# A larger allowed lateness for the planned order of VectorE and ScalarE in a four-layer graph kernel

## The chip, the cores and the metric

The kernel runs on one core of one Trainium2 chip. The metric is the device time of one execution in microseconds, as the median over the runs of one kernel. The profile comes from one further execution. In it PE is TensorE's matmuls, PEld its weight loads, DVE is VectorE, ACT is ScalarE, POOL is GpSimd and SP the engine that issues most of the loads.

## The reference

The input is x (4096 x 64) and adj (4096 x 4096, about one entry in 128 is 1, the others 0). Four graph layers follow each other, each as `x = x + layer(relu(layernorm(x)), adj)`:

```python
# layer 0: weights from the rank of a neighbour in its row
out = w @ (h @ weight) + bias          # w = mask * 0.5 ** (k - pos) where pos > 0
# layer 1: attention
h, q, k = lorentz_linear(...)           # 64 columns each
att = adj * sigmoid((2 + 2 * qm @ k.T) / att_scale + att_bias)
support = att @ h
out = support / sqrt(|-inner(support)|)
# layer 2: two gated graph convolutions, each with m = adj @ (x @ W)
# layer 3: hyperbolic: num = A @ (gamma * X), den = A @ (gamma - 1), alpha = sum(A),
#          then norms, artanh and tanh per row
```

## The kernel before

**A fast and a general program.** `fast_kernel` holds adj as 8-bit floats in on-chip memory for all four layers (tiles `A8`), which is exact only if every entry is 0 or 1. Whether that is so is tested as the kernel runs: the generator `checks` loads 128 pieces of adj of 128 x 1024 in 32-bit floats (`whole`, 512 KB each; the first few are shared with the conversion to 8 bits), and one VectorE instruction for each piece counts entries that are neither 0 nor 1 (a scalar_tensor_tensor with an accumulator, which the trace lists as a second, short instruction, DVE_READ_ACCUMULATOR). Every 16 tests their counts are added up; behind the last one a matmul `flag_ps` and a copy make the `flag`, and only if it is above 0 does `general_kernel` run afterwards. The tests can stand anywhere before the end; nothing but the reading of the flag at the end waits for their values.

**The planner.** The order of the instructions is written by a small planner, `Weave`, while the program is built. It keeps a planned clock for every engine (`weave.t`), books every instruction with a cost (`Engine.cost`: on VectorE 0.13 us plus 1.09 ns an element, 0.08 more with an accumulator) and remembers when each tile is ready. The main line of the program, scores, sums and evacuations, is issued directly (`V`, `S_`); side work is given as generators (`DV`, `AC`) that are put in where there is room. Side work is in `weave.work`, of which the first two pieces are looked at; the tests are in `weave.back`, which is looked at after those and not at all while `weave.quiet` is set. Two places put side work in:

- `fill`, called before each direct instruction of VectorE and ScalarE: an operation goes ahead of it if its planned end is not after the moment at which the direct one is ready, plus `weave.late`.
- `draw`, called between groups of matmuls: an operation of VectorE or ScalarE is issued if its planned end is at most 0.4 us plus `weave.late` past TensorE's planned clock.

```python
if self.e in "DA":
    w.fill(self.e, w.ready(self.e, ins, outs) + w.late)      # a direct instruction, L791

go = begin + op.dur <= now + self.LAG["P"] + self.late       # draw, L726
```

**Layer 0** (`stream0`) and the first quarter of layer 1 come first, to about 308 us in the trace. **Layer 1's corner part** is the function `rest` in `stream1`: for three quarters q of the rows and two halves c, 16 steps i, 96 steps in all. A step is four score matmuls of a 64 x 64 corner (`score4`), two sigmoids on ScalarE and one multiply by adj on VectorE (`weigh`, tile `sig`), and four matmuls that sum (`sum4`); the sums of a step are issued behind the scores of the third step after it. `sig` and `whole` share six buffers (`b4`). In this part `depth[0]` is 1: the load of one further piece is issued when a test is. Beside it runs the post-processing of the quarter before (`post1`: row statistics, layer norm, splits), as side work.

**Layer 2** (`layer2`, two convolutions, 475 to about 677 us) is planned with `depth[0]` 4 and takes tests where VectorE has room, until `weave.quiet` is set ahead of the last evacuation. **Layer 3** (`layer3`) sums eight units of 512 rows. It begins with the halves that are ready; when the last S tiles are there (`DONE` has (4, NQ - 1)) all tests that are left are issued at once, ahead of everything else on VectorE:

```python
weave.quiet = False
while weave.back and weave.back[0][1].e == "D":
    weave.issue(weave.back[0])
```

Then each unit is evacuated (`take3`), its row statistics are made (`head3`), and norms, artanh and tanh follow (`post3`): for units 3 to 5 and 0 to 2 in groups of three, for units 6 and 7 singly. `last3` does unit 7, after which nothing is left for TensorE. Helpers record nearly all operations, so L785 in the profile is any operation of the planner's engines, and L984 any matmul.

Of the kernel before, what the change touches and what calls it, by code (L numbers as in the profile page):

```python
# [796 lines left out]
def fast_kernel(ctx: ExitStack, tc: tile.TileContext, t: dict, out: bass.AP, flag: bass.AP):  # L797
# [24 lines left out]
    weave = Weave()  # L822
    free = weave.free

    def one(name):
        return weave.take(1, lambda: psp.tile([P, CW], F32, tag="one", name=name, bufs=8))

    def several(names_):
        return [one(n) for n in names_]

    def b2(name, shape=(P, QB, D), dtype=F32):
        return b2p.tile(list(shape), dtype, tag="b2", name=name)
# [148 lines left out]
    def mm(o, lhsT, rhs, start=True, stop=True):  # L981
        weave.wait(names(lhsT, rhs), names(o))
        book_pe(o, lhsT, rhs, 4 if lhsT.dtype == F32 else 1)
        nc.tensor.matmul(o, lhsT, rhs, start=start, stop=stop, skip_group_check=True)  # L984
# [340 lines left out]
    def load1(q):  # L1325
        if q < NQ:
            qd[q] = [b2("qd", (P, CW)) for _ in range(2)]
            for c in range(2):
                for half in (slice(0, D), slice(D, P)):
                    Y_.dma_start(qd[q][c][half, :], q_spill[q][c * D:(c + 1) * D, :])  # L1330

    def score(q, i, c):

        kb = kT[i // 4][:, (i % 4) * P:(i % 4 + 1) * P]
        ps = several(("score", "score"))
        for j in range(2):
            half = slice(j * D, (j + 1) * D)
            mm(ps[j], kb[half, :], qd[q][c][half, :])
        return ps
# [3 lines left out]
    def score4(q, i, c):  # L1343

        kb = kT[i // 4][:, (i % 4) * P:(i % 4 + 1) * P]
        ps = several(("score", "score"))
        for j, (r, h) in enumerate(corners):
            mm(ps[j // 2][h, :], kb[r, h], qd[q][c][r, :])
        return ps

    def sum4(acc, i, g):

        for k, (r, h) in enumerate(corners):
            b = 2 * i + k % 2
            mm(acc[k // 2][h, :], S1[b // QB][r, b % QB, :], g[r, k % 2, :],
               start=i == 0, stop=i == NB // 2 - 1)

    def weigh(q, i, c, ps):

        g = b4p.tile([P, 2, CW], F32, tag="b4", name="sig")  # L1360
        for j in range(2):
            S_.activation(g[:, j, :], ps[j], AF.Sigmoid, bias=att_add, scale=att_mul)
            free(ps[j])
        v = g.rearrange("p k (j n) -> p k j n", n=P)
        a = A8[q][i].rearrange("p k (j c n) -> p k c j n", c=2, n=P)[:, :, c]
        V.tensor_tensor(v, v, a, ALU.mult)
        return g
# [9 lines left out]
    def stream1():  # L1377

        acc, behind = [], []

        def add(c, q, i, gs):
            if i == 0:
                acc.append(one(f"acc{c}"))
            for j in range(2):
                b = 2 * i + j
                mm(acc[c][j * D:(j + 1) * D, :], S1[b // QB][:, b % QB, :], gs[c][:, j, :],
                   start=i == 0, stop=i == NB // 2 - 1)

        def add_behind(more=()):
            q, i, gs = behind.pop(0)  # L1390
            for c in (0, 1):
                add(c, q, i, gs)
                if more:
                    more.pop(0)()
                weave.draw(weave.quiet)

        def turn(q, i, later=None):
            if q == 0 and i % (QB // 2) == 0:
                weave.until((1, i // (QB // 2)), DONE)
            weave.quiet = (1, NQ - 1) not in DONE  # L1400
            weave.late = 2.0 if weave.quiet else 0.8
            gs = ahead[:] if (q, i) == (0, 0) else []
            for c in range(len(gs), 2):
                ps = score(q, i, c)
                if later is None:
                    gs.append(weigh(q, i, c, ps))
                else:
                    later.append(lambda q=q, i=i, c=c, ps=ps: gs.append(weigh(q, i, c, ps)))
                weave.draw(weave.quiet or c == 1)
            behind.append((q, i, gs))  # L1410
            if i == 8:
                load1(1)

        def rest():

            q0, i0, gs = behind.pop(0)

            def last():
                add(1, q0, i0, gs)
                weave.finish()  # L1420
                weave.add(post1(q0, acc[:]))
                acc.clear()

            sums = [lambda: add(0, q0, i0, gs), last]

            def close(q, c, ps):
                if c == 0:
                    halves[q] = b2("agg", (P, CW))
                    weave.add(evac4(halves[q], ps, c))
                else:  # L1430
                    weave.finish()
                    weave.add(post1(q, ps))

            def sums_of(q, c, i, g):
                if i == 0:
                    acc[:] = several(("acc0", "acc1"))
                sum4(acc, i, g)
                if i == NB // 2 - 1:
                    close(q, c, acc[:])
                    acc.clear()  # L1440

            def pop():
                sums.pop(0)()
                weave.draw()

            for q in range(1, NQ):
                for c in (0, 1):
                    for i in range(NB // 2):
                        g = weigh(q, i, c, score4(q, i, c))
                        weave.draw(False)  # L1450
                        sums.append(lambda q=q, c=c, i=i, g=g: sums_of(q, c, i, g))
                        if len(sums) > 3:
                            pop()
                        if (c, i) == (1, 0):
                            load1(q + 1)
            while sums:
                pop()

        for q in range(1):
            for i in range(0, NB // 2, 2):  # L1460

                later = []
                turn(q, i)
                turn(q, i + 1, later)
                while len(behind) > 2:
                    add_behind(later)
                for go in later:
                    go()
                if len(behind) > 1:
                    add_behind()  # L1470
        weave.until((1, NQ - 1), DONE)
        weave.quiet, weave.late = False, 0.8
        rest()

    X, halves = {}, {}
# [1 line left out]
    def evac4(a, acc, c):  # L1477

        own, other = [slice(0, D), slice(D, P)][::1 - 2 * c]
        t = b2("mt", (P, CW))  # L1480
        yield AC.activation(t, acc[0], AF.Copy)
        free(acc[0])
        yield DV.tensor_tensor(t, acc[1], t, ALU.add)
        free(acc[1])
        yield AC.activation(a[own, :], t[other, :], AF.Copy)
        yield DV.tensor_tensor(a[own, :], t[own, :], a[own, :], ALU.add)

    def post1(q, acc):
        if q in halves:
            a = halves[q]  # L1490
            yield from evac4(a, acc, 1)
        else:
            a = yield from evac(acc)
        X[q] = b2(f"X{q}")
        yield SY.dma_start(flat(X[q]), x_spill[q])
        sup = b2("sup")
        ps = yield from to_nm(a)
        sq = b2("sq")
        yield AC.activation(sq, ps, AF.Square)
        yield AC.activation(sup, ps, AF.Copy)  # L1500
        free(ps)
        s = stat("space", QB)
        yield DV.tensor_reduce(s, sq[:, :, 1:], AX.X, ALU.add)
        yield DV.tensor_tensor(s, s, sq[:, :, 0], ALU.subtract)
        a = stat("abs", QB)
        yield DV.tensor_scalar(a, s, -1.0, 1e-8, op0=ALU.mult, op1=ALU.max)
        yield DV.tensor_tensor(s, s, a, ALU.max)
        r = yield from rsqrt(s)
        yield DV.tensor_tensor(sup, sup, rows(r), ALU.mult)
        yield DV.tensor_tensor(X[q], X[q], sup, ALU.add)  # L1510

        g = b2("g0")
        yield from relu_ln(X[q], g)
        yield from split3(g, 1.0, *parts(2, q), psum=False)
        DONE.add((2, q))
        gT = b2("gT", (P, CW))
        yield from transpose4(g, gT)
        yield from spill2(q, 0, gT)
# [443 lines left out]
    lead[0] = math.inf  # L1962
    depth[0] = 1
    stream1()
    depth[0] = 4
    for step in range(2):
# [89 lines left out]
```

## Time and profile before

| | |
|---|---|
| median of the runs | 793.5 us (793.33 to 793.5) |
| the profiled execution, its own time | 794.03 us |
| its span in the trace | 792.2 us |
| PE busy | 751.9 us (95%) |
| DVE busy | 636.0 us (80%) |
| ACT busy | 435.8 us (55%) |
| tests of adj on VectorE | 128 |
| granted TensorE clock, mean | 0.989 |

The span is what the trace covers; the profiled execution's own time holds 1.8 us more around it. Busy shares are means over stages that differ: in the slices of the page TensorE stands at nine tenths or more nearly throughout, and VectorE between five and nine tenths.

### The profile page before, as it was taken

The page shows a single profiled execution, that of the slowest core. Times are in us where ns is not written, and L with a number is a line of the kernel's source. Part 1 is how long each engine was busy: PE and PEld are TensorE (multiplying, and loading weights), DVE is VectorE, ACT ScalarE, POOL GpSimd, SP SyncE. Part 2 cuts the span into 40 slices and gives each one's busy share as a digit, 9 for nine tenths or more (in the row PEclk, how much of TensorE's full clock was granted, in tenths as well). Part 3 has the DMA queues.
Part 4 walks back from the last instruction along what each step waited for, and adds up shares of the span by engine and source line. Part 5 has one row for each costly group of instructions (what it writes and reads, how often), then busy time and mean ns, then how long its engine had stood idle before and what let it go on. Part 6 is the DMA issues. An engine that isn't in the chain of part 4 may idle for free.

```text
span 792.2 us, 13872 instructions
## 1 busy us (share of the span) xinstructions
PE 751.9 (95%) x5241; PEld 364.6 (46%) x5262; DVE 636.0 (80%) x1442; ACT 435.8 (55%) x765; POOL 62.0 (8%) x129
## 2 busy tenths in 40 slices
PE   6899999999999999999999999999999999999980
PEld 2334444444543433333333334434444354899980
DVE  5886867778779888998988988857978688768886
ACT  5555556555557678898899882041220345532243
POOL 4332232231000000000000000000000000000000
PEclk9999999999999999999999999999999999999995
DMA  9999999999610013010010027987779620003001
GB/s 202 155 188 178 222 164 193 222 164 207 202 49 26 14 67 94 1 55 28 2 54 1 2 65 235 321 252 245 257 258 363 188 80 28 1 2 134 2 22 37
DMA packets 44106, 98.64 MB, mean 125 GB/s; under 512 B 5120, under 2 KB 20608, under 8 KB 44032
## 3 DMA queue, kind: packets, MB, share of 16 engines
q1 hardware_dynamic: 25888, 78.98, 29.2%
q0 software_dynamic: 15984, 14.56, 19.6%
q10 hardware_dynamic: 2160, 4.14, 1.4%
q8 instruction: 43, 0.70, 0.4%
q14 instruction: 31, 0.25, 0.1%
HBM read 136.06 MB, written 5.24 MB: 178 GB/s over the span
## 4 chain that ended last, share of the span: by engine, by line
PE 79%; DVE 12%; ACT 3%; DMA 2%; issue 2%; SPq 0%; ACTq 0%; DVEq 0%
PE acc L984 47%; PE score L984 13%; PE cnt L984 12%; DVE n L785 2%; PE rz L984 2%; DVE ss L785 2%; PE ps_l L984 1%; DMA whole<-in_adjT 1%; PE ps_t L988 1%; DVE whole L785 1%; DVE sig L785 1%; DVE nt L785 1%; PE ih L984 1%; ACT sig L785 1%; DMA x<-in_x 1%
## 5 line engine op out<-in xcount | busy, mean ns | idle before, releaser
L785 ACT ACTIVATE sig<-score,fatt_add,fatt_mul 128x512 f32<-128x512 f32 x256 | 182.8, 776 | 31.4 <-PE score L984 25.6
L785 DVE TENSOR_TENSOR sig<-sig,A 128x1024 f32<-128x1024 f32 x128 | 155.2, 1222 | 24.2 <-ACT sig L785 22.3
L785 ACT ACTIVATE w<-cnt 128x512 int16<-128x512 f32 x198 | 111.4, 595 | 90.2 <-PE cnt L984 87.4
L785 DVE SCALAR_TENSOR_TENSOR whole<-whole 128x1024 f32<-128x1024 f32 x128 | 153.0, 1218 | 9.4 <-DMA whole<-in_adjT 8.8
L984 PE MATMUL acc<-sig,S 64*64 64x512 f32 (+1 forms) x896 | 130.8, 592 | 1.4 <-DVE sig L785 1.2
L984 PE MATMUL score<-qd,kT 64*64 64x512 f32 (+1 forms) x896 | 131.6, 594 | 0.0
L984 PEld LDWEIGHTS <-hm 128*128 128x128 bf16 x768 | 73.5, 98 | 92.5 <-issue 9.3
L984 PE MATMUL acc<-A,hm 128*128 128x512 fp8e4 x512 | 115.2, 379 | 0.0
L984 PE MATMUL cnt<-A,ftri 128*128 128x512 fp8e4 x256 | 97.4, 383 | 7.1 <-ACT A L785 5.8
L984 PE MATMUL cnt<-A,fupd 128*128 128x512 fp8e4 x248 | 94.8, 382 | 5.7 <-DVE w L785 2.1
L984 PE MATMUL acc<-S,A 128*128 128x196 bf16 x1024 | 88.5, 246 | 1.3 <-DVE S L785 1.3
L984 PEld LDWEIGHTS <-A 128*128 128x128 fp8e4 x1024 | 87.0, 97 | 2.2 <-DVE S L785 1.5
L984 PEld LDWEIGHTS score<-qd,kT 64*64 64x64 f32 (+1 forms) x896 | 41.1, 140 | 67.6 <-issue 57.5
L785 DVE TENSOR_SCALAR w<-cnt 128x512 int16<-128x512 f32 x58 | 40.1, 691 | 39.9 <-PE cnt L984 38.5
L984 PE MATMUL acc<-w,hm 128*128 128x512 bf16 x235 | 70.4, 379 | 1.2 <-DVE hm L785 0.4
L984 PEld LDWEIGHTS acc<-sig,S 64*64 64x64 f32 (+1 forms) x896 | 36.8, 133 | 74.9 <-issue 47.7
L868 POOL DMA_DIRECT2D A<-in_adjT x111 | 59.9, 542 | 127.2 <-DMA A<-in_adjT 126.0
L984 PEld LDWEIGHTS <-lo 128*64 128x64 bf16 x768 | 39.6, 109 | 49.3 <-issue 18.5
L984 PE MATMUL acc<-A,lo 128*64 128x512 fp8e4 x512 | 57.9, 380 | 0.0
L785 ACT ACTIVATE mt<-acc 64x512 f32<-64x512 f32 (+1 forms) x32 | 19.0, 592 | 64.1 <-PE acc L984 63.6
L984 PEld LDWEIGHTS <-ftri 128*128 128x128 bf16 x256 | 24.8, 98 | 45.5 <-issue 21.4
L984 PEld LDWEIGHTS <-fupd 128*128 128x128 bf16 x248 | 24.3, 98 | 37.9 <-issue 13.3
(190 smaller groups left out, 618.2 us busy)
## 6 DMA issues: line engine op xcount, KB each, us to landing
whole<-in_adjT SPq DMA_DIRECT2D x128, 512.0 KB, 6.8
A<-in_adjT POOLq DMA_DIRECT2D x111, 128.0 KB, 13.7
qd<-qs SPq DMA_DIRECT2D x16, 128.0 KB, 3.7
mx<-gs SPq DMA_DIRECT2D x16, 128.0 KB, 8.4
xT<-gs SPq DMA_DIRECT2D x8, 256.0 KB, 7.5
x<-in_x SPq DMA_DIRECT2D x6, 256.0 KB, 6.1
xs<-x SPq DMA_DIRECT2D x4, 256.0 KB, 5.9
qs<-qT ACTq DMA_DIRECT2D x4, 256.0 KB, 4.6
```

Of the source, the lines that this page charges most:

```text
L785: return fn(*args, **kw)
L868: nc.gpsimd.dma_start(A8[q][b // 2][:, b % 2, :], a)
L984: nc.tensor.matmul(o, lhsT, rhs, start=start, stop=stop, skip_group_check=True)
L988: nc.tensor.transpose(o, src, ident)
```

## The change

One number. After the first quarter of layer 1, and before the corner part begins, `weave.late` is set to 1.2 instead of 0.8. It is not set again, so the value holds for everything that is planned after that line, the corner part, layer 2 and layer 3. What the engines compute is the same; only the order in which VectorE's and ScalarE's instructions stand, and with it that of the loads of `whole`, can differ.

```diff
         weave.until((1, NQ - 1), DONE)
-        weave.quiet, weave.late = False, 0.8
+        weave.quiet, weave.late = False, 1.2
         rest()
```

## The prediction

> **What bounds the kernel now.** I read the busy times stage by stage first, then TensorE's waits, then the chain that ended last, then VectorE's timeline in two places.
>
> The stages (start and end in us; busy us of PE, PEld, DVE, ACT, POOL, each with its count; clock; DMA share; GB/s) are the corner part, the last tests with the sums beside them, the rest of layer 3, and what follows TensorE's last matmul:
>
> ```profile
> 308.00:475.00 167.00, 167.00 (x1540) 59.67 (x1532) 148.92 (x203) 150.02 (x219) 0.00 (x0) 1.00 0.09 27
> 719.70:736.00 16.30, 15.61 (x182) 15.28 (x182) 14.27 (x28) 1.03 (x6) 0.00 (x0) 1.00 0.47 162
> 736.00:769.90 33.90, 33.89 (x398) 33.62 (x397) 30.62 (x138) 12.40 (x46) 0.00 (x0) 1.00 0.04 14
> 769.90:792.20 22.30, 0.00 (x0) 0.00 (x0) 15.06 (x89) 9.31 (x21) 0.00 (x0) 0.61 0.10 33
> ```
>
> See in it: TensorE is never idle in the corner part, while VectorE has 18 us to spare there. At the end it is the reverse: TensorE stops at 769.9 and VectorE works on. The same table for the instructions on `whole` (DVE alone; two counts are one test) says where the tests of adj run: 3 in the corner part, 66 from 475 to 640, 1 to 719.7, and 11 from 719.7 to 736:
>
> ```profile
> 308.00:475.00 167.00, 3.68 (x6) 0.00 (x0) 0.00 (x0) 1.00 0.09 27
> 475.00:640.00 165.00, 78.89 (x132) 0.00 (x0) 0.00 (x0) 1.00 0.76 255
> 640.00:719.70 79.70, 1.23 (x2) 0.00 (x0) 0.00 (x0) 1.00 0.09 28
> 719.70:736.00 16.30, 12.95 (x22) 0.00 (x0) 0.00 (x0) 1.00 0.47 162
> ```
>
> TensorE's waits from 470 us on (total, times, longest):
>
> ```profile
> PE acc L984 <- DVE S L785: 1.3, 1, 1.3
> PE flag_ps L984 <- DVE n L785: 0.7, 1, 0.7
> PE acc L984 <- DVE sig L785: 0.2, 1, 0.2
> ```
>
> So TensorE itself can gain little. The chain of waits shows what the last tests cost (start, us, what):
>
> ```profile
> 719.24 0.84 DVE S L785 x2
> 720.08 5.16 DVE whole L785 x9
> 725.24 0.48 issue
> ...
> 725.83 7.71 DMA whole<-in_adjT
> 733.63 1.24 DVE whole L785 x2
> ```
>
> From 719.2 the chain runs over VectorE almost without a break to the end: the 11 tests hold it from 719.99 to 734.89, 14.9 us with 1.9 us of waits for loads, and everything that layer 3 wants from it is late by that much. The first sums' addition, `n<-n,acc`, ready before 724, runs at 735.18.
>
> VectorE in the corner part, where no post-processing runs:
>
> ```profile
> 416.38 1.23 DVE L785 TENSOR_TENSOR sig<-sig,A 128x1024 f32<-128x1024 f32 x1 [0.49 <-ACT sig L785]
> 418.10 1.23 DVE L785 TENSOR_TENSOR sig<-sig,A 128x1024 f32<-128x1024 f32 x1 [0.49 <-ACT sig L785]
> 419.81 1.23 DVE L785 TENSOR_TENSOR sig<-sig,A 128x1024 f32<-128x1024 f32 x1 [0.49 <-ACT sig L785]
> ```
>
> A step is 1.717 us, and 0.49 us idle stands in front of every multiply, with no test in any gap.
>
> [...]
>
> **The change, step by step.**
>
> (1) *Why 0.8 lets no test in.* A test is put before a multiply if its planned end is at most `late` past the moment the multiply is ready. Planned: test 0.13 + 1.09e-3 x 1024 + 0.08 = 1.326 us, multiply 1.246, step on TensorE 8 x 0.215 = 1.72, two sigmoids 1.32. VectorE is then free 1.72 - 1.246 = 0.474 us before the multiply (0.49 in the trace, so the plan holds). A test needs 1.326 - 0.8 = 0.526: just too much, in every step. With 1.2 it needs 0.126.
>
> (2) *How many go in.* After a test VectorE is 0.852 behind, then 0.378, then 0.096 ahead (under 0.126), then 0.474 again: one test in three steps. Walking over the idle gaps of the corner part in the trace (16.2 us behind the sigmoids, in 39 gaps) with 1.33 us a test, I get 12 places; post-processing that is pushed back, and tests that were there anyway, take some. I take **10 more (6 to 12)**.
>
> (3) *What they cost there.* Each adds 1.15 us to VectorE (its start-to-start time, 719.99 to 721.14), in idle time. The multiply behind it is up to 0.7 us late (1.15 less the gap). Who waits for that: sums of a step are issued behind the scores of the third step after it. The multiply of 356.52 ends at 357.75, its sums start at 359.97: 2.2 us to spare, so nothing until the last steps. There the last multiply is waited for already (0.2 us); one test in front adds up to 0.7. I take +0.5. Each test also issues one load on SP's queue, past the q and x loads of the next parts, which are asked for 27 us or more before use, and holds one of six `b4` buffers as the one waiting test does now. DMA is at 0.09 there; loads land in 4.1 to 4.6 us, and three steps are 5.15. Cost nothing, unless they land late (rival D).
>
> (4) *What is gone later.* Layer 2 fills what room it has (66 tests), so the ten come off the end of the line: of the last 11 one is left (0 to 5). Ten are 11.5 us of VectorE; the load waits of 1.9 go too, as the first of that group were loaded ahead. TensorE's wait at `flag_ps` goes: -0.7.
>
> (5) *The tail.* With VectorE in time, what remains behind TensorE's end is the last unit's own chain. Now it loses: 1.35 us, as its evacuation stands behind logarithms and a table load on ScalarE (the addition is at 771.70, possible at 770.35); 5.3 us between its row statistics (773.35) and its reciprocal (778.68), which earlier units fill; and 2.1 us, as 778.68 to 786.85 is shared with unit 6, where alone it is some 23 small operations of 0.16 to 0.2, a logarithm pair 0.5, a table load with its dummy 1.5, and the last products 1.1: about 6.1. Together 8.7. Is there room? Without tests VectorE's work from 719.7 on is 14.27 - 12.95 + 30.62 + 15.06 = 47.0 us, in 49.5 us up to TensorE's end and about 8 after it, but units 6 and 7 come late; I keep back 2.2 of the 8.7. So -6.5.
>
> (6) *0.4 us outlives the corner part.* `late` is set nowhere afterwards. In layers 2 and 3 operations of ScalarE and VectorE may stand 0.4 us longer before a direct evacuation. TensorE has other sums beside it except before layer 3's second half (the 1.3 us wait). Bounds -1.3 to +3; I take -0.3, as the chain that is waited for is the one moved forward.
>
> Sum: +0.5 - 0.7 - 6.5 - 0.3 = **-7.0**. The profiled execution took 794.03 (span 792.2), so 787.0; the median before is 0.5 below that execution, so 786.5.
>
> **The rivals.** A is the above: 6 tests fewer at the end give about -5, all 11 with the whole tail -9.4: 784 to 789.
>
> B, *the chain before layer 3's second half becomes the bound*: the Tanh of the last gates (684.93) now just precedes a logarithm table load (685.64). If the order flips it waits to 690.03, 5 us; some 3 arrive at TensorE: 789.5 (788.5 to 792). For it: TensorE already waits there. Against: more lateness issues such operations earlier.
>
> C, *it doesn't do what it says*: gaps too small or tests displaced one for one: 793.5. Against: 0.474 against 0.126 isn't close.
>
> D, *slower*: the loads land late in the corner part. A waiting test stands before multiplies on VectorE's in-order queue, sums wait behind those. It happened before: at 288.75 a load of 3.81 us is in the chain, with two tests and a multiply behind it. It decides from 5.15 + 2.2 - 0.7 = 6.7 us to landing; at 7.7 (the longest in the last stage) each of ten tests costs TensorE 1.0: +10 - 7 = 796.5. Against: 4.1 to 4.6 us in this stage.
>
> **How the numbers follow.** A 0.58, B 0.14, C 0.08, D with smaller losses of order 0.20. Faster by over 0.2% (about what a measurement of this kernel can tell from no change): A and B, 0.72; within: 0.08; slower: 0.20. The likeliest, A, gives 786.5, alone 784 to 789. The range runs from 783.5 (A's floor) to 796.5 (D's price), leaving out about one in seven.
>
> **What would show it.** Right: 9 to 15 tests between 308 and 475, spaced three steps where multiplies stand alone; 0 to 5 after 719; `n<-n,acc` following its sums within 2 us; reciprocal to last X about 6 us; no flag_ps wait. Wrong: VectorE waits for `whole` loads in the corner part, TensorE waits for `sig` there beyond the last steps, the wait for `S` above 1.3, or an unchanged tail though the tests are gone.

## The result, and the profile after

| | before | after |
|---|---|---|
| median of the runs, us | 793.5 (793.33 to 793.65) | 786.64 (786.02 to 787.04) |
| ratio to before, 95% interval | | 0.9913 [0.9896, 0.993] |
| the profiled execution, us | 794.03 | 786.02 |
| its span, us | 792.2 | 784.2 |
| tests of adj: corner part / from there to 719.7 / behind that | 3 / 67 / 11 | 9 / 69 / 3 |

The change saves 6.9 us between medians, 8.0 between the two profiled executions. The forecast was 786.5.

The stages of the profile after, read as before (start and end in us; busy us of PE, PEld, DVE, ACT, POOL; clock; DMA share; GB/s):

```profile
308.00:475.00 167.00, 167.00 (x1532) 61.29 (x1532) 153.98 (x213) 148.72 (x219) 0.00 (x0) 1.00 0.14 43
719.70:736.00 16.30, 16.30 (x194) 16.10 (x192) 14.05 (x49) 4.45 (x17) 0.00 (x0) 1.00 0.01 1
736.00:769.90 33.90, 33.50 (x395) 33.27 (x392) 29.87 (x143) 13.79 (x43) 0.00 (x0) 1.00 0.08 25
769.90:784.20 14.30, 0.00 (x0) 0.00 (x0) 7.80 (x48) 4.54 (x13) 0.00 (x0) 0.62 0.07 23
```

VectorE has 5.1 us more to do in the corner part and 7.3 us less behind TensorE's end. TensorE stops at 769.5 (769.9 before), so nearly all of the gain is in what follows it, which I call the tail: 22.3 us before, 14.7 now. The same table for `whole` alone (DVE only; two counts are one test; the ninth test of the corner part, at 474.20, runs across 475 and is counted in both rows):

```profile
308.00:475.00 167.00, 10.61 (x17) 0.00 (x0) 0.00 (x0) 1.00 0.14 43
475.00:640.00 165.00, 80.85 (x136) 0.00 (x0) 0.00 (x0) 1.00 0.77 262
640.00:719.70 79.70, 2.45 (x4) 0.00 (x0) 0.00 (x0) 1.00 0.05 15
719.70:736.00 16.30, 3.52 (x6) 0.00 (x0) 0.00 (x0) 1.00 0.01 1
```

Six tests moved into the corner part and two into layer 2. Where multiplies stand alone in the corner part, there is a test every third step. VectorE's timeline in a stretch without post-processing (start, us, engine, operation, form; in brackets what ended an idle time):

```profile
355.64 1.22 DVE L785 SCALAR_TENSOR_TENSOR whole<-whole 128x1024 f32<-128x1024 f32 x1
356.79 0.08 DVE L785 DVE_READ_ACCUMULATOR whole<-whole 128x1 f32 x1
356.79 1.22 DVE L785 TENSOR_TENSOR sig<-sig,A 128x1024 f32<-128x1024 f32 x1
358.45 2.56 DVE L785 TENSOR_TENSOR sig<-sig,A 128x1024 f32<-128x1024 f32 x2 [0.44 <-ACT sig L785]
360.93 1.22 DVE L785 SCALAR_TENSOR_TENSOR whole<-whole 128x1024 f32<-128x1024 f32 x1
```

A test, three multiplies, a test: 5.29 us from one to the next, three steps. The idle 0.49 us that stood in front of every multiply is left once in three (0.44).

TensorE's waits from 300 us to the end:

```profile
PE acc L984 <- DVE sig L785: 1.0, 1, 1.0
PE acc L984 <- DVE r L785: 0.3, 1, 0.3
```

The waits for `S` (1.3) and at `flag_ps` (0.7) are gone; the wait for `sig`, which is the end of the corner part, grew from 0.2 to 1.0. That list does not hold all that TensorE loses. Its first scores of the corner part and its first sums of layer 2, before and after:

```profile
304.59 1.95 PE L984 MATMUL score<-qd,kT 64*64 64x512 f32 x16
...
476.83 3.63 PE L984 MATMUL acc<-A,hm 128*128 128x512 fp8e4 x16
```

```profile
304.12 1.95 PE L984 MATMUL score<-qd,kT 64*64 64x512 f32 x16
...
477.64 3.63 PE L984 MATMUL acc<-A,hm 128*128 128x512 fp8e4 x16
```

Between the two the traces have 1568 matmuls each, of the same kinds. They take 172.24 us before and 173.52 after, 1.28 us more, of which the list has 0.75. The starts also differ, by 0.47 us, although TensorE, VectorE and ScalarE have the same order up to there; over all kernels below they lie between 303.90 and 305.32. So a place in one profile is compared with the same place in another to about 1 us only, and the length of a stage is the better measure.

The chain that ended last, which ran over VectorE's tests from 719.2 on, now stays on TensorE there:

```profile
715.98 9.10 PE acc L984 x107
725.08 0.12 PE flag_ps L984 x2
```

And the end, VectorE's timeline (unit 7's last addition, its reciprocal, the last product):

```profile
770.87 0.48 DVE L785 TENSOR_TENSOR n<-n,acc 128x65 f32<-128x65 f32 x2
...
773.41 0.17 DVE L785 RECIPROCAL rc<-den 128x4 f32<-128x4 f32 x1
...
778.54 0.42 DVE L785 TENSOR_TENSOR X<-X,n 128x256 f32<-128x256 f32 x1
```

### The profile page after: what moved, and what is told of

Its sections match the earlier page's. It is cut to its first block, busy times and chain, and to the rows that moved or that the text cites. A ratio compares the mean times of both kernels' runs of the same rounds, so it can differ in the third digit from the quotient of the medians.

```text
span 784.2 us, 13883 instructions
## 1 busy us (share of the span) xinstructions
PE 755.4 (96%) x5262; PEld 366.5 (47%) x5262; DVE 636.6 (81%) x1442; ACT 435.5 (56%) x765; POOL 61.7 (8%) x129
## 4 chain that ended last, share of the span: by engine, by line
PE 84%; DVE 6%; ACT 4%; DMA 3%; issue 2%; POOL 1%; ACTq 0%; DVEq 0%; POOLq 0%
PE acc L984 52%; PE cnt L984 13%; PE score L984 12%; ACT sig L785 2%; DMA A<-in_adjT 2%; PE rz L984 2%; PE ps_l L984 1%; DVE sig L785 1%; PE ps_t L988 1%; PE ih L984 1%; ACT w L785 1%; DVE ss L785 1%; PE ps_kq L984 1%; DVE whole L785 1%; DVE n L785 1%
## 5 line engine op out<-in xcount | busy, mean ns | idle before, releaser
L984 PE MATMUL acc<-w,hm 128*128 128x512 bf16 x256 | 75.4, 379 | 0.0
```

## The experiments

My theory after the result: tests that are left ahead of layer 3's second half lengthen the tail behind TensorE, so the six tests in the corner part carry the gain. One rival: the new lateness in layers 2 and 3 carries it, and the corner part does little. Another: `late` is a dial on which more is better. Differences below are from the runs of before that stood beside each experiment (medians 793.8 to 794.0).

**The corner part alone, and the rest alone.**

```diff
-        weave.quiet, weave.late = False, 1.2
-        rest()
+        weave.quiet, weave.late = False, 1.2     # e1_corner_only
+        rest()
+        weave.late = 0.8
```

> Lateness 1.2 in the corner part alone, 0.8 again from layer 2 on. The order then has 9 tests in the corner part, as with the whole change, but 7 are left for the start of layer 3's second half (11 before, 3 with the whole change). Theory (what counts is how many tests stand ahead of layer 3's last work on VectorE, some 0.85 us each, from 793.5 with 11 and 786.6 with 3): about 790, half of the gain. Rival 1 (tests in the corner part are the gain, wherever the others go): 787, nearly all of it. Rival 2 (the gain is the new order in layers 2 and 3 under the larger lateness): 793 to 794.

```diff
-        weave.quiet, weave.late = False, 1.2
-        rest()
+        weave.quiet, weave.late = False, 0.8     # e2_later_only
+        rest()
+        weave.late = 1.2
```

> Lateness 0.8 in the corner part as before, 1.2 from layer 2 on. The corner part keeps its 3 tests, 8 are left for layer 3's second half. Theory (0.85 us for each test left): about 791. Rival 1 (tests in the corner part are the gain): 793.5. Rival 2 (the order in layers 2 and 3): 787.

Measured: e1 791.21, ratio 0.9967 [0.9955, 0.998], 2.6 us faster. e2 790.02, ratio 0.9952 [0.9938, 0.9965], 3.8 us faster. Together that is 6.4 of the 6.9. So neither is the whole: the part for which I had taken a gain of 0.3 us is the larger one. TensorE's waits from 300 us on, of e1:

```profile
PE acc L984 <- DVE S L785: 1.3, 1, 1.3
PE acc L984 <- DVE sig L785: 1.0, 1, 1.0
```

and of e2:

```profile
PE acc L984 <- DVE r L785: 0.3, 1, 0.3
PE acc L984 <- DVE sig L785: 0.2, 1, 0.2
```

e1 has the nine tests in the corner part, waits 1.0 at its end, and keeps the wait for `S`; e2 has three tests there, waits 0.2, and has lost the wait for `S`. The tests left over at the end are 7 in e1 and 8 in e2, against 11 and 3. The row of the windows table for `whole` in e2, where the last tests stand:

```profile
719.70:736.00 16.30, 9.22 (x16) 0.00 (x0) 0.00 (x0) 1.00 0.20 65
```

**The threshold.** A test needs a lateness of 1.326 - 0.474 = 0.852. Both kernels fall back to 0.8 behind the corner part.

```diff
+        weave.quiet, weave.late = False, 0.84    # e3_084 (0.86 in e4_086)
         rest()
+        weave.late = 0.8
```

> Lateness 0.84 in the corner part, 0.8 afterwards. A test needs 1.326 - 0.84 = 0.486, more than the planned 0.474: 3 tests in the corner part and 11 at the end as before. Theory: 793.5, unchanged, 0.02 below the value that moves tests. If lateness acted gradually: some tenths less.

> Lateness 0.86 in the corner part, 0.8 afterwards. The planned gap is 0.474 and a test needs 1.326 - 0.86 = 0.466, so tests go in: 8 in the corner part, 7 left at the end. Theory: about 790, the same as with 1.2 in the corner part alone within 0.7 us, since only the threshold counts. If the size of the lateness counted beyond the threshold: near 793.

Measured: 0.84 gives 794.1, ratio 1.0002 [0.9995, 1.0009], with 3 tests in the corner part and 11 left, as before. 0.86 gives 790.54, ratio 0.996 [0.9946, 0.9973], with 8 and 7. The threshold lies between them as worked out, and 0.86 already gives what 1.2 gives to the corner part (e1: 791.21), with a corner part that is 0.65 us shorter (172.81 us, e1 173.46).

**Leaving tests out.** If a test left over at the end is what costs, then leaving out the last 11 tests, at the old lateness, must gain all of it.

```diff
+        todo = todo[:-11]      # e5_117: before; e6_after_125: after, with [:-3]
```

> The kernel before with the last 11 pieces of adj left untested (117 tests of 128), lateness 0.8 throughout; this leaves out part of the computation of the flag. Nothing is moved into the corner part; the group of tests ahead of layer 3's second half is just gone. Theory (that group is the cost): as fast as the changed kernel or faster, 784.5 to 786.5, with the last chain after TensorE's end as short as there. Rivals (the gain comes from the corner part or from the order under the larger lateness): 792.5 to 793.5.

> The changed kernel with its last 3 pieces left untested (125 of 128), which are the 3 that still stand ahead of layer 3's second half; part of the flag's computation is left out. If the tail is already down to the last unit's own chain (the prediction's floor): 786 to 786.6, nothing more to gain. If each test there still costs 0.85: 784.

Measured: e5 790.6, ratio 0.9957 [0.9943, 0.997]; e6 787.88, ratio 0.9923 [0.991, 0.9936]. Both miss. e5's tail is 15.1 us, as short as expected, but the time isn't. TensorE's waits from 300 us on, and e5's row of the windows table for `whole`, of which the clock counts here (third number from the end):

```profile
PE acc L984 <- DVE S L785: 3.7, 1, 3.7
PE acc L984 <- DVE sig L785: 0.2, 1, 0.2
```

```profile
719.70:736.00 16.30, 0.00 (x0) 0.00 (x0) 0.00 (x0) 0.90 0.00 1
```

TensorE waits 3.7 us for `S` in place of 1.3 and ends at 773.2 in place of 769.9. Of these 3.3 us the wait is 2.4, and the wait at `flag_ps` that is gone takes off 0.7. The 1.6 left fit the clock: the granted clock of TensorE is 0.90 in this row, where before has 1.00, and 10% of 16.3 us is an estimated 1.6 us. Sums are slow straight behind the wait: the first 29 there take 3.97 us, where 28 of the same kind take 2.54 in after (both in the timelines below). The other profiles with this row (before, after, e1, e2 and e6 to e10b) have 1.00 in it, and before and e1 wait 1.3 us for `S`. e3 and e4 wait as long, and their sums behind the wait take 0.088 us each, as in before. That the wait of 3.7 us lowered the clock is not shown: the two stand together in one execution.

So my theory fell as the whole cause: a second term stands beside the tail, the wait ahead of layer 3's second half, and it moves with the planned order.

e6 has none left and is 1.2 us slower than after by medians (two sets of runs, the intervals overlap). It spends the same time on TensorE from the first corner scores on; its tail is 1.1 us longer. Of that, 0.9 is seen: ScalarE's table load of 1.28 us stands at 770.59 and unit 7's evacuation behind it at 772.00, so that the addition comes 2.24 us behind TensorE's end in place of 1.36. e9 below has the same (769.01, 770.42).

**What the wait for S depends on.** TensorE's timeline around layer 2's end shows it. `ps_l` is the last product that TensorE makes for a quarter's `S`; `ps_o` brings the last quarter's update of x back into rows; `acc<-S,A` are layer 3's sums over the halves that are ready, which fill the time. Before:

```profile
682.22 1.08 PE L984 MATMUL ps_l<-W,h3T 128*128 128x128 f32 x8
683.13 16.48 PE L984 MATMUL acc<-S,A 128*128 128x196 bf16 x192
699.46 0.60 PE L988 MATMUL ps_o<-fident,xT 128*128 128x128 f32 x4
...
708.15 1.08 PE L984 MATMUL ps_l<-W,h3T 128*128 128x128 f32 x8
709.07 9.35 PE L984 MATMUL acc<-S,A 128*128 128x196 bf16 x108
719.73 6.45 PE L984 MATMUL acc<-S,A 128*128 128x196 bf16 x73 [1.31 <-DVE S L785]
```

After:

```profile
686.16 1.08 PE L984 MATMUL ps_l<-W,h3T 128*128 128x128 f32 x8
687.08 2.54 PE L984 MATMUL acc<-S,A 128*128 128x196 bf16 x28
689.46 0.60 PE L988 MATMUL ps_o<-fident,xT 128*128 128x128 f32 x4
...
708.02 1.08 PE L984 MATMUL ps_l<-W,h3T 128*128 128x128 f32 x8
708.93 16.14 PE L984 MATMUL acc<-S,A 128*128 128x196 bf16 x188
```

And e5, from the last `ps_l` on:

```profile
710.76 1.08 PE L984 MATMUL ps_l<-W,h3T 128*128 128x128 f32 x8
711.68 6.96 PE L984 MATMUL acc<-S,A 128*128 128x196 bf16 x80
722.34 3.97 PE L984 MATMUL acc<-S,A 128*128 128x196 bf16 x29 [3.70 <-DVE S L785]
```

From the start of the filling sums to the first sum that needs the new `S` it is 719.73 - 709.07 = 10.66 us before and 722.34 - 711.68 = 10.66 us in e5: the chain of post-processing took the same time in both, and TensorE bridges it with the sums that it has not yet used. Before had 108 of them left, 9.35 us; e5 had 80, 6.96 us. 10.66 - 9.35 and 10.66 - 6.96 are the two waits, 1.31 and 3.70.

In after, `ps_o` stands 28 sums behind the third quarter's `ps_l` rather than 192, and the two `ps_l` are 21.86 us apart rather than 25.93: 48 fewer sums are spent between them. As 24 more are spent ahead of the third quarter's gates (64, 40 before), 24 are gained. That leaves 132 at the last `ps_l`, an estimated 11.4 us at 0.0866 us each (9.35 us for 108), more than the 10.66 of the chain. What brought `ps_o` forward is seen on VectorE: the three operations that update x stand ahead of the quarter's row statistics in after (686.33 to 688.47), and behind them in before (689.99 to 698.29).

e1, e3 and e4 are like before here: 108 sums left, a wait of 1.31. All other kernels with more than 0.8 behind the corner part (e2, e6 to e9, e10 and e10b) have `ps_o` early and no wait. Where e5 differs from before is also to be read: between its third quarter's gates and `ps_l` (676.92 to 684.49, 7.57 us; before 4.75) TensorE spends 32 more of these sums, 8 fewer ahead of the gates and 4 more behind `ps_l`, which makes the 28 that it lacks. That the sigmoid of those gates stands behind a table load 3.3 us later (679.17; before 675.82) fits it, but wasn't tested.

**Is it the lateness, or that tests are missing?**

```diff
+        todo = todo[:-11]      # e9_117_later12: before, and
         rest()
+        weave.late = 1.2
```

> Lateness 0.8 in the corner part, 1.2 from layer 2 on, and the last 11 pieces of adj untested (117 of 128; part of the flag's computation is left out). So no test is moved into the corner part, none stands ahead of layer 3's second half, and layers 2 and 3 are ordered under the larger lateness. Theory of two terms (7.6 us of tail from the tests that are gone, 1.3 us of TensorE's wait for S from the later order): no wait for S, a tail of about 15 us, 785.5 to 787, as the changed kernel or a little better, since the last multiply of the corner part isn't delayed. Rival (the wait of 3.7 us for S that came when the 11 tests were dropped is caused by their absence, whatever the lateness): about 790, as without the larger lateness.

Measured: 785.91, ratio 0.9902 [0.9886, 0.9918]. TensorE's only wait from 300 us on:

```profile
PE acc L984 <- DVE sig L785: 0.2, 1, 0.2
```

The same 117 tests as e5, 4.7 us faster, and the wait for `S` is gone; the clock from 719.7 to 736 is 1.00. So the lateness behind the corner part takes the wait away. It shows the other half as well: with no test added to the corner part and none left at the end, the time is that of after (786.64; the intervals overlap). The tests in the corner part are worth what they take off the end, less what they cost there, and nothing by themselves.

**More of it.**

```diff
-        weave.quiet, weave.late = False, 1.2
+        weave.quiet, weave.late = False, 1.6     # e7_late16; 2.0 in e8_late20
```

> Lateness 1.6 in place of 1.2: 11 tests in the corner part, none left for layer 3's second half. Theory: 785 to 786.6, limited by the end of the corner part, where the last multiply waits for a test, and by the last unit's chain. Rival (lateness eats TensorE's 2.2 us of margin in the corner part): over 787, with TensorE waiting for sig there.

> Lateness 2.0 in place of 1.2: 14 tests in the corner part, none left at the end, 3 spare places more. Theory: no better than with 1.6, since the tail has nothing more to give: 785 to 787. Rival (margin of 2.2 us is gone): 788 or more, TensorE waiting for sig in the middle of the corner part.

Measured: 1.6 gives 786.73, ratio 0.9908 [0.9895, 0.992]: no test is left at the end, the tail is 14.7 us, the same as with three left, and the time equals after. 2.0 gives 788.86, ratio 0.9935 [0.9923, 0.9948], 2.1 us slower than 1.6 in the same set of runs: 14 tests in the corner part, which takes 175.78 us, 3.5 more than before and 2.2 more than with 1.6. The tail is 14.9. So the dial has a best place: what is gained at the end stops when the tail has reached its floor, and past it the corner part pays. Two of the waits in there are named, one of 0.57 us at its end (before 0.22) and this one in its middle:

```profile
438.82 1.09 PE L984 MATMUL acc<-sig,S 64*64 64x512 f32 x8 [0.50 <-DVE sig L785]
```

The rest comes in several pieces of 0.2 to 0.7 us; which wait each of them is stays open.

**Taking back the 0.8 us at the corner part's end.** No tests in its last three steps, with 1.2 and with 1.6:

```diff
+        weave.quiet = (q, c) == (NQ - 1, 1) and i > 12   # in rest, ahead of weigh
         ...
         rest()
+        weave.quiet = False
```

> The changed kernel, with no test put into the last three steps of the corner part: 8 tests there, 4 left for layer 3's second half. Theory: TensorE's wait for the last multiply falls from 1.0 to 0.2 us, the tail stays at 14.7 to 15.5: 785.5 to 786.5. If four left tests already bring back part of the tail (19.1 us with 7): 787 to 788.

> Lateness 1.6 in place of 1.2, and no test in the last three steps of the corner part: 10 tests there, none left for layer 3's second half. Theory: last multiply waited for 0.2 us, no wait for S, tail 14.7: 785.5 to 786.2, the best of all, 0.5 to 1 under the changed kernel. If the order under 1.6 makes another chain late (TensorE's wait for S comes back): 787 or more.

Measured: with 1.2, 787.98, ratio 0.993 [0.9915, 0.9944], a miss; with 1.6, 785.31, ratio 0.9895 [0.9879, 0.9911], a hit and the fastest of all full computations. The wait at the corner part's end is 0.3 and 0.2 again, and the corner part is 0.7 us shorter than in after and 0.6 shorter than in e7. But with 1.2 the one test taken out of the corner part is a fourth at the end, and the tail grew from 14.7 to 17.1. Its VectorE timeline there:

```profile
774.02 0.17 DVE L785 RECIPROCAL rc<-den 128x4 f32<-128x4 f32 x1
...
775.03 0.42 DVE L785 TENSOR_TENSOR X<-X,n 128x256 f32<-128x256 f32 x1
...
780.16 0.42 DVE L785 TENSOR_TENSOR X<-X,n 128x256 f32<-128x256 f32 x1
```

Unit 6's product comes at 775.03, behind unit 7's reciprocal, and the two share VectorE; in after unit 6's stands at 773.07, ahead of it. In e1 they share it to the end, with products at 782.56 and 783.55. By these three timelines the tail falls in steps and not test by test: what counts is whether unit 6 is through when unit 7 comes. Against after, e10b is 1.3 us faster by medians, in another set of runs; the two intervals overlap, so that it beats after is likely and not certain.

All together, from the profiles (us):

| kernel | left at the end | corner part | wait for S | PE's end | tail |
|---|---|---|---|---|---|
| before | 11 | 172.24 | 1.3 | 769.9 | 22.3 |
| e3, 0.84 | 11 | 172.24 | 1.3 | 770.8 | 22.3 |
| e2, later only | 8 | 172.24 | 0 | 769.3 | 19.1 |
| e1, corner only | 7 | 173.46 | 1.3 | 770.3 | 19.0 |
| e4, 0.86 | 7 | 172.81 | 1.3 | 769.0 | 19.1 |
| e10, quiet, 1.2 | 4 | 172.79 | 0 | 768.9 | 17.1 |
| after | 3 | 173.52 | 0 | 769.5 | 14.7 |
| e10b, quiet, 1.6 | 0 | 173.05 | 0 | 768.6 | 14.6 |
| e7, 1.6 | 0 | 173.61 | 0 | 769.0 | 14.7 |
| e8, 2.0 | 0 | 175.78 | 0 | 771.6 | 14.9 |
| e6, three left out | 0 | 173.51 | 0 | 770.1 | 15.8 |
| e9, eleven left out | 0 | 172.24 | 0 | 768.5 | 15.8 |
| e5, eleven left out | 0 | 172.24 | 3.7 | 773.2 | 15.1 |

The tail follows the tests left at the end: 22.3 with 11, about 19.1 with 7 or 8, 17.1 with 4, and a floor of 14.6 to 15.8 with three or none. The corner part takes the same time to 0.01 us in the five kernels with three tests in it, and 0.6 to 3.5 us more where tests were added. PE's end also holds where the corner part started (303.90 to 305.32), which differs from one execution to the next though the order up to there is the same: of the 0.9 us between before and e3, 0.45 stood there already, and 0.4 is a longer wait at `flag_ps`.

## Why the prediction was right, point by point

The time is right and the main mechanism too: VectorE's work at the end goes, and the tail shortens. But steps 2 to 6 were mis-sized, in both directions, and part of the agreement is luck, as they cancel.

**Step 1, the threshold: right**, shown from both sides by 0.84 and 0.86.

**Step 2, ten more tests: six.** The range 6 to 12 held it. The spacing was right, and so were the places in the three bare stretches (about 355 to 367, 412 to 423, 469 to 474). The step failed where post-processing runs: I walked over the idle gaps of the trace there, of 0.3 to 0.5 us, and the planner does not see them. In its costs a step with a further operation of 512 elements has 1.246 + 0.688 = 1.93 us of VectorE in 1.72, no room at all.

**Step 3, +0.5 for the last multiply: +1.3 for the corner part, +0.75 of it there.** The corner part's end in VectorE's timeline of after, with TensorE's line:

```profile
474.20 1.22 DVE L785 SCALAR_TENSOR_TENSOR whole<-whole 128x1024 f32<-128x1024 f32 x1
...
475.35 1.22 DVE L785 TENSOR_TENSOR sig<-sig,A 128x1024 f32<-128x1024 f32 x1
...
476.62 1.09 PE L984 MATMUL acc<-sig,S 64*64 64x512 f32 x8 [0.97 <-DVE sig L785]
```

A test, the last multiply, and the sums 0.05 us later: the place was named rightly, and two of the added tests fall in the last five steps. e10 and e10b, where the wait is 0.3 and 0.2 again, show the cause. What failed is the "nothing until the last steps": TensorE loses 0.5 us earlier, which stays in e10, and by another path than the margin of 2.2 us (see the last section).

**Step 4, one test left: three.** That follows from step 2 (four fewer), less two that layer 2 took in, which I had at none. The wait at `flag_ps`, -0.7, went as said.

**Step 5, the tail: -6.5 forecast, -7.6 measured**. The sum is 1.1 short, and its parts were:

| part | loss before, as forecast | gained |
|---|---|---|
| PE's end to unit 7's addition | 1.35 | 0.44 (1.8 to 1.36) |
| addition to reciprocal | 5.3 | 4.4 (6.98 to 2.54) |
| reciprocal to the last X | 2.1 | 2.6 (8.17 to 5.55) |
| kept back for want of room | -2.2 | |

Two thirds of the first part stayed, because a table load still stands ahead of that evacuation, 1.28 us with 0.20 for a dummy activation behind it, as in before (770.00 and 771.29). ScalarE's timeline of after:

```profile
768.88 1.28 ACT L785 ACT_TABLE_LOAD   x1
...
770.28 0.21 ACT L785 ACTIVATE n<-acc 128x65 f32<-128x65 f32 x1
```

The reciprocal comes 0.9 us behind unit 7's row statistics, with unit 6's last product in between, so that nearly all of the second part came back. Unit 6 is then through at 773.50, ahead of that reciprocal's work, and the last unit has VectorE alone: 5.55 us, not 6.1. So the 2.2 held back for want of room were the mis-sized term: there was room, with three tests still in front.

**Step 6, the lateness behind the corner part: -0.3 forecast, with -1.3 as its lower bound; the bound itself came.** This is the term that failed most in kind: I wrote that TensorE's wait for `S` might move, gave the direction, and took almost nothing. It is gone in every kernel with more than 0.8 behind the corner part, and in none with 0.8. With it belong the two tests that layer 2 took in addition. By e2 this step is worth 3.8 us, more than half of the whole, because with three tests fewer at the end the tail is 3.2 us shorter as well. A new wait of 0.3 us for `r` in layer 2 takes a little of it back.

The measured terms are +1.3 - 0.7 - 7.6 - 1.3 + 0.3 = -8.0, as between the profiles. That it comes out so even is chance: the profile after began its corner part 0.5 us earlier, and 0.4 us from layer 2 to TensorE's end, against what the waits give, stays open.

**The rivals.** B's place was the right one to look at: the chain before layer 3's second half is what the lateness moves. It moved the other way, and something near B's price (2.4 us more there, B had 3) came only in e5. It did not come by the flip that B named: the Tanh (687.19) stands ahead of the logarithm load (687.91) in e5 too. D did not come: loads in the corner part land in 3.7 to 4.5 us, VectorE never waits for one. C is refuted by the tests' places.

**What was to be seen:** 9 to 15 tests in the corner part (9), 0 to 5 at the end (3), reciprocal to last X about 6 us (5.55), no wait at `flag_ps`: all came. The first sums' addition was to follow its sums within 2 us. With three tests still in front it just misses that: evacuated at 721.71, added at 723.72, 2.01 us later.

```profile
723.72 1.14 DVE L785 TENSOR_TENSOR n<-n,acc 128x130 f32<-128x130 f32 x4
```

That delay costs nothing that the table can show: with no test in front (e7, e10b) the tail is the same.

## What to carry to other kernels

When an order is planned, count how much goes into a gap with the planner's own costs and thresholds; the gaps that the trace shows are not the gaps that it sees. Work that can stand anywhere should be off the stage at whose end its engine is the last to work (the tail was 22.3 us with 11 tests left there, 14.7 with 3), and it is enough to move so much that the tail reaches its floor; the last tests moved gained nothing here (14.7 with none left) and cost at the place where they went (a corner part of 175.78 us with 14 tests, 173.61 with 11). A setting that is never reset is a second change in every later stage: split it by stage before crediting the place it was meant for, and look at how much filling work is left in front of each wait, since the length of the dependent chain, less that stock, was the wait to a hundredth of a microsecond. And measure a stage by the distance between the same two instructions in both profiles: busy time and the list of waits showed 0.75 of the 1.28 us here.

## What the runs showed that I had not expected

ScalarE pays for the tests, and TensorE pays for that where no list shows it. In the corner part of after the sigmoids wait for `whole` 5.7 us in 7 times, as the two share six buffers; the view of the tile `whole` in the corner part lists who waited for it:

```profile
  ACT sig L785: 5.7, 7
```

TensorE's list has no wait for it. But two of these waits, of 0.64 and 0.56 us, stand here in ScalarE's timeline:

```profile
367.53 2.12 ACT L785 ACTIVATE sig<-score,fatt_add,fatt_mul 128x512 f32<-128x512 f32 x3 [0.64 <-DVE whole L785]
...
424.17 2.12 ACT L785 ACTIVATE sig<-score,fatt_add,fatt_mul 128x512 f32<-128x512 f32 x3 [0.56 <-DVE whole L785]
```

Behind each, two of the four score matmuls of a step begin later than the other two, by 0.3 us around 370 and by 0.2 us around 427 (a step's scores, eight records in the trace, take 1.33 and 1.25 us, 1.04 ahead of it), and beside both the weight loads of scores have one wait of 0.3 us for ScalarE's `sig`. The early and the late pair run beside each other, so TensorE counts as busy, 167.00 of the 167.00 us from 308 to 475. From the next `ps_n` on (372.81 and 429.45), a matmul of 128 x 128, the four start together again, and everything behind it is 0.3 us later than before, and 0.2 more the second time. That is the 0.5 us that step 3 lacked. The places fit; no run here takes these waits away while leaving the tests. With 14 tests in that part (e8) the sigmoids' waits are 7.0 us up to 475, 7.9 up to layer 2, and TensorE falls behind more.
